# A mask's table moved ahead of a LayerNorm's power on GpSimd, and a PSUM copy moved ahead of exponentials on ScalarE

## The chip, the cores and the metric

One core of one Trainium2 chip. The metric is the device time of one launch in microseconds (us), median of several runs. Where a kernel is compared with another by a ratio, both ran on the same chip in the same rounds. A ratio is the mean time of one kernel's runs over that of the other's of the same rounds, so it is not quite the ratio of the medians quoted beside it.

## The reference, cut to what matters

128 graphs with 128 nodes and 512 features go through two layers, each with a residual and a LayerNorm: a graph attention with 8 heads and a mask from the adjacency, then two hypergraph convolutions with a LayerNorm between them.

```python
# layer 0: attention
dense = leaky_relu(e_self[..., :, None] + e_neigh[..., None, :], 0.2)
dense = dense + NEG_BIG * (1.0 - A[:, None, :, :])       # the mask: 0 or -1e10
att = softmax(dense, axis=-1)
x = layernorm(x + relu(att @ feats + b))                  # "first LayerNorm"
# layer 1: hypergraph convolutions
h = layer_norm(relu(hypergraph_conv(x, adj, W1, b1)))     # "first convolution"
x = layernorm(x + hypergraph_conv(h, adj, W2, b2) + x)
```

## The kernel before

The kernel takes graphs in 64 pairs. Each step of a pair has a lag (in turns of the loop) and a time within the turn; all steps of all pairs are sorted by `(pair + lag) * 38.6 + time`, and every engine gets its instructions in that order. So a turn mixes work of five pairs (lags 0 to 4). What the change and the argument touch:

```python
    @step(0, 38.4)                                   # GpSimd: the mask's table, once per pair
    def mask(p, s):
        s["neg"] = work.tile([P, 2, N], F32, tag="neg", name=f"neg_{p}", bufs=2)
        nc.gpsimd.tensor_scalar(s["neg"], s["a"], -1.0, BIG, op0=ALU.add, op1=ALU.mult)
    ...
    for (g, q), tm, (lag, tl), (lagx, tx), te, tt in (
        ((0, 0), 31.0, (1, 33.2), (1, 36.1), 2.7, 18.1), ((0, 1), 32.2, ..., 4.6, 18.15),
        ((1, 0), 34.2, ..., 7.8, 21.5), ((1, 1), 35.4, ..., 7.9, 21.55),
    ):
        at(1, tm, masked, g, q)                      # GpSimd: scores += neg   ("nb", L576)
        at(2, te, exponential, g, q)                 # ScalarE: 4 exponentials ("nb", L606)
    ...
    # GpSimd: h_means 30.62 ("m"), rstds "a" 30.8 (first LayerNorm's power, "rsa"),
    #         h_rstd 36.0 (second power, "rsh"), z_sums 2.7, 3.4, 4.1, 4.8 ("zS", L780)
    # VectorE: y_scale 0.6 and 1.3 (two SBUF inputs, "y<-y,rsh,bw_bc", L909)
    ...
    # TensorE, first convolution as seven products; X, Y, W are PSUM banks:
    # product 1 -> X (2.0), 2 -> Y (3.8), 6 adds into X (5.6), 5 -> W (7.35), 7 adds into X ...
    # product 6 reads zS[1]; copy 0 empties X (ScalarE, 4.0, L329) before product 6 adds into it
    chain("ph", 3, (2.0, 3.8, 5.6, 7.35, 9.1, 12.65, 14.4, 4.0, 7.5, 11.0), hidden, HALF)
```

## Time and profile before

| | before |
|---|---|
| time, median of 3 runs | 2561.94 us (2559.85 to 2563.33) |
| span of the profiled run, clock granted to TensorE (1 is full speed) | 2559.9 us, 0.997 |
| TensorE matmul / weight loads busy | 98% / 89% |
| one turn of the loop | 39.21 us |
| stall of TensorE in a turn, by starts of weight loads | 0.56 us |

Read it as a kernel whose TensorE is almost full, with one short wait that returns in 61 of the 64 turns. That the wait matters shows in part 4 of the page, the chain that ended last (the work followed back from the last instruction, at each step to what released it): TensorE is only two thirds of it, and GpSimd has a quarter.

```profile
PE 66%; POOL 23%; issue 8%; DVE 2%; DMA 1%; ACT 0%; SPq 0%; POOLq 0%; DVEq 0%; ACTq 0%
```

### The profile page before, as it was taken

What the parts mean: (1) busy time and instruction counts of PE and PEld (TensorE: products, weight loads), DVE (VectorE), ACT (ScalarE), POOL (GpSimd) and SP (SyncE); (2) the same over time, 40 slices, a digit from 0 to 9 for tenths busy, and PEclk for the clock granted to TensorE, in tenths of its full rate; (3) what the DMA queues carried; (4) which work ended last, traced back from release to release, by engine and by line L of the source; (5) the groups of instructions that cost most, each with busy time, mean ns of one, the idle gap of its engine ahead of it and who ended that gap; (6) DMA issues with size and microseconds to landing.
All of it is one profiled execution on the core that took longest, in us unless ns stands there. A gap on an engine that the chain in (4) does not pass through costs nothing.

```text
span 2559.9 us, 48549 instructions
## 1 busy us (share of the span) xinstructions
PE 2516.7 (98%) x16349; PEld 2275.8 (89%) x16349; DVE 1914.3 (75%) x4332; ACT 1539.8 (60%) x4481; POOL 1832.7 (72%) x2058
## 2 busy tenths in 40 slices
PE   7999999999999999999999999999999999999998
PEld 5899889998998998989989988999899999898997
DVE  7877777777777777777777777777777777777765
ACT  4565665655756656657556566565575665665753
POOL 5777777776777677767777777777677767776774
PEclk9999999999999999999999999999999999999999
DMA  6544444444444444454454444444444444444431
GB/s 184 134 137 134 135 139 141 134 125 145 129 133 141 133 141 135 127 150 130 126 147 133 134 136 138 141 134 124 147 128 133 141 133 141 136 130 148 130 108 54
DMA packets 420840, 343.76 MB, mean 134 GB/s; under 512 B 141272, under 2 KB 370160, under 8 KB 420592
## 3 DMA queue, kind: packets, MB, share of 16 engines
q1 hardware_dynamic: 417120, 336.19, 44.4%
q10 hardware_dynamic: 3472, 4.47, 0.5%
q8 instruction: 131, 2.15, 0.3%
q14 instruction: 117, 0.96, 0.1%
HBM read 238.83 MB, written 101.71 MB: 133 GB/s over the span
## 4 chain that ended last, share of the span: by engine, by line
PE 66%; POOL 23%; issue 8%; DVE 2%; DMA 1%; ACT 0%; SPq 0%; POOLq 0%; DVEq 0%; ACTq 0%
PE phX L792 14%; POOL nb L576 11%; PE pyX L473 9%; PE phW L792 9%; PE pfX L473 9%; PE pav L662 8%; POOL zS L780 4%; PE pq L919 4%; PE pyY L473 4%; PE pfW L473 4%; POOL neg L363 2%; PE pfY L473 2%; POOL rsh L905 2%; POOL rsa L709 2%; DVE y L876 1%
## 5 line engine op out<-in xcount | busy, mean ns | idle before, releaser
L792 PEld LDWEIGHTS phX<-zS,w_sb 128*128 128x128 f32 x3072 | 362.8, 192 | 61.5 <-issue 31.1
L792 PE MATMUL phX<-zS,w_sb 128*128 128x128 f32 x3072 | 380.7, 277 | 19.0 <-POOL zS L780 17.2
L329 ACT COPY py<-pyX 128x257 f32<-128x257 f32 x189 | 70.8, 375 | 539.2 <-PE pyX L473 526.4
L845 POOL TENSOR_TENSOR sq<-sq 128x512 f32<-128x512 f32 (+2 forms) x384 | 343.9, 896 | 23.7 <-ACT sq L833 0.5
L576 POOL TENSOR_TENSOR nb<-nb,neg 128x512 f32<-128x512 f32 x256 | 318.2, 1275 | 13.5 <-DMA nb<-rd 13.5
L592 ACT ACTIVATE nb<-nb,ft 128x128 f32<-128x128 f32 x1020 | 317.7, 391 | 6.8 <-POOL nb L576 6.8
L606 ACT ACTIVATE nb<-nb,nm 128x128 f32<-128x128 f32 x1024 | 319.9, 393 | 0.4 <-DVE nm L598 0.4
L598 DVE TENSOR_REDUCE nm<-nb 128x4 f32<-128x512 f32 x256 | 174.6, 683 | 179.5 <-ACT nb L592 117.4
L709 POOL TENSOR_TENSOR rso<-veo,mhalf 128x2 f32<-128x2 f32 x63 | 44.1, 700 | 332.9 <-DVE veo L707 332.9
L662 PEld LDWEIGHTS pav<-ft,eT 128*128 128x128 f32 x2048 | 248.3, 192 | 8.4 <-DVE eT L639 0.8
L662 PE MATMUL pav<-ft,eT 128*128 128x65 f32 x2048 | 242.5, 272 | 0.0
L473 PE MATMUL pyX<-w_sb,hS 128*128 128x257 f32 x1008 | 242.5, 382 | 0.0
L473 PE MATMUL pyX<-w_sb,h 128*128 128x257 f32 x1008 | 239.5, 379 | 0.5 <-ACT py L329 0.5
L822 ACT ACTIVATE h<-h,vecs 128x128 f32<-128x128 f32 x768 | 238.4, 392 | 2.2 <-DVE h L807 2.2
L473 PE MATMUL pyW<-w_sb,hS 128*128 128x256 f32 x1008 | 238.6, 378 | 0.3 <-DVE y L876 0.3
L473 PEld LDWEIGHTS pyW<-w_sb,hS 128*128 128x128 f32 x1008 | 190.7, 189 | 27.9 <-DVE y L876 0.7
L686 POOL TENSOR_TENSOR y<-y,b_bc 128x512 f32<-128x512 f32 x128 | 162.5, 1270 | 67.6 <-DVE y L677 67.6
L473 PEld LDWEIGHTS pyX<-w_sb,h 128*128 128x128 f32 x1008 | 186.4, 190 | 25.5 <-ACT py L329 0.9
L473 PEld LDWEIGHTS pyX<-w_sb,hS 128*128 128x128 f32 x1008 | 186.1, 190 | 24.3
L627 DVE STREAM_TRANSPOSE eT<-eb 128x512 f32<-128x512 f32 x252 | 163.1, 684 | 0.8 <-DMA eb<-ed 0.7
L833 ACT ACTIVATE sq<-h 128x512 f32<-128x512 f32 x256 | 160.7, 629 | 2.1
L455 POOL TENSOR_TENSOR hS<-h 128x512 f32<-128x512 f32 x126 | 158.6, 1277 | 2.3 <-ACT h L822 2.3
(167 smaller groups left out, 5669.2 us busy)
## 6 DMA issues: line engine op xcount, KB each, us to landing
nb<-rd SPq DMA_DIRECT2D x127, 512.0 KB, 6.6
ed<-nb SPq DMA_DIRECT2D x126, 512.0 KB, 2.6
eb<-ed SPq DMA_DIRECT2D x504, 128.0 KB, 2.9
x<-in_x_dram SPq DMA_DIRECT2D x64, 512.0 KB, 9.4
out_dram<-o SPq DMA_DIRECT2D x63, 512.0 KB, 2.8
xb<-in_x_dram SPq DMA_DIRECT2D x248, 128.0 KB, 3.0
a<-in_adj_dram SPq DMA_DIRECT2D x64, 128.0 KB, 8.1
w<-in_adj_dram SPq DMA_DIRECT2D x128, 64.0 KB, 7.4
```

What stands on the lines that cost most here:

```text
L473: nc.tensor.matmul(to[:, :n], lhs[:, k, :], rhs[:, k, :n], start=bool(start) and k == 0, stop=(k == nk - 1), skip_group_check=True,)
L576: nc.gpsimd.tensor_tensor(t, t, neg[:, :, None, :].to_broadcast([P, NB, HH, B]), op=ALU.add)
L592: nc.scalar.activation(t, t, AF.Prelu, bias=s["ft"][:, g, h, 0:1], alpha=SLOPE)
L598: nc.vector.tensor_reduce(s["nm"][:, g, hs], scores(p, s, g, hs).rearrange("p b h j -> p h b j"), AX.XY, ALU.max, negate=True,)
L606: nc.scalar.activation(t, t, AF.Exp, bias=s["nm"][:, g, h:h + 1])
L627: nc.vector.transpose(s["eT"][:, g, hs, :].rearrange("p h (b i) -> p h b i", b=NB), s["eb", g][:, :, hs, :].rearrange("p b h j -> p h b j"),)
L662: nc.tensor.matmul(t[:, h * (U + 1):(h + 1) * (U + 1)], s["eT"][:, g, q * HH + h, :], s["ft"][:, g, q * HH + h, 2:], start=True, stop=True,)
L686: nc.gpsimd.tensor_tensor(s["y"][:, g, :], s["y"][:, g, :], b0_bc, op=ALU.add)
L792: nc.tensor.matmul(to[:, m * N:(m + 1) * N], w[:, k, m * P:(m + 1) * P], rhs[:, k, :], start=bool(start) and m == 0 and k == 0, stop=(k == ...
L822: nc.scalar.activation(dst[:, k, :], src[:, k, :], AF.Relu, bias=b1_sb[:, c:c + 1])
L833: nc.scalar.activation(s["sq"][:, g, q * KH // 2:(q + 1) * KH // 2, :], hid(s, g, q), AF.Square, scale=DH ** -0.5,)
L845: nc.gpsimd.tensor_tensor(t[:, :n, :], t[:, :n, :], t[:, n:2 * n, :], op=ALU.add)
```

## The change

The intent: the mask's table is not urgent, yet it stood between the second power and the differences zS for which TensorE waits. It goes into a gap in which GpSimd waits anyway. And the copy that the same TensorE product needs no longer stands behind four exponentials.

```diff
-    @step(0, 38.4)
+    @step(0, 30.63)
     def mask(p, s):
...
-        ((0, 0), 31.0, (1, 33.2), (1, 36.1), 2.7, 18.1), ...
+        ((0, 0), 31.0, (1, 33.2), (1, 36.1), 4.05, 18.1), ...
```

More of the change, by code (lines that the diff above doesn't have):

```diff
@@ L643 @@
     for (g, q), tm, (lag, tl), (lagx, tx), te, tt in (
-        ((0, 0), 31.0, (1, 33.2), (1, 36.1), 2.7, 18.1), ((0, 1), 32.2, (1, 35.0), (1, 36.7), 4.6, 18.15),
+        ((0, 0), 31.0, (1, 33.2), (1, 36.1), 4.05, 18.1), ((0, 1), 32.2, (1, 35.0), (1, 36.7), 4.6, 18.15),
         ((1, 0), 34.2, (2, 2.05), (2, 2.1), 7.8, 21.5), ((1, 1), 35.4, (2, 6.0), (2, 7.3), 7.9, 21.55),
```

## The prediction

> **What bounds the kernel now.** I read the page first, then the table of waits, then the chain that ended last, then the timeline of one steady turn of the loop (64 pairs of graphs; one turn is 39.21 us, from the chain's step to GpSimd's mask at 1314.26 us to the same step at 1353.47). Part 1 of the page:
>
> ```profile
> PE 2516.7 (98%) x16349; PEld 2275.8 (89%) x16349; DVE 1914.3 (75%) x4332; ACT 1539.8 (60%) x4481; POOL 1832.7 (72%) x2058
> ```
>
> TensorE (PE, with its weight loads PEld) is the bound; the question is only where it still stands. The table of waits (total us, times, longest) names one wait that returns every turn, and beside it an engine that has time to spare:
>
> ```profile
> PEld phX L792 <- POOL zS L780: 28.8, 61, 0.5
> POOL rsa L709 <- DVE vea L707: 151.1, 64, 3.3
> ```
>
> The first: in 61 turns TensorE waits for the difference that GpSimd (POOL) makes (zS). The second: GpSimd itself sat idle 2.36 us in the mean (151.1 / 64) before the first LayerNorm's power. The chain that ended last (start us, length us, what) joins the two:
>
> ```profile
> 1304.54 0.34 POOL m L894 x2
> 1304.88 2.37 issue
> ...
> 1307.28 0.70 POOL rsa L709
> 1307.98 2.17 POOL nb L576 x2
> ...
> 1314.26 0.96 POOL neg L363
> 1315.22 1.14 POOL zS L780
> ...
> 1316.43 0.74 POOL zS L780
> ...
> 1317.21 2.05 PE phX L792 x16
> ```
>
> So GpSimd idles 2.37 us, makes the power, adds the mask four times, makes the second power, then the next pair's mask table (neg, 0.96 us), and only then the two differences for which TensorE stands. The loads of weights in the timeline show how long it stands (start us, length, then the group):
>
> ```profile
> 1313.09 1.86 PEld L792 LDWEIGHTS phX<-zT,w_sb 128*128 128x128 f32 x16
> 1314.87 1.87 PEld L792 LDWEIGHTS phY<-zT,w_sb 128*128 128x128 f32 x16
> 1317.21 1.86 PEld L792 LDWEIGHTS phX<-zS,w_sb 128*128 128x128 f32 x16 [0.48 <-POOL zS L780]
> 1318.99 1.87 PEld L792 LDWEIGHTS phW<-zS,w_sb 128*128 128x128 f32 x16
> ```
>
> Like groups start 1.78 us apart (1314.87 - 1313.09, 1318.99 - 1317.21), these two 2.34. **The stall is 0.56 us a turn**; the 0.48 in brackets is less, since ends are modelled. Over 61 turns it is 34 us, 1.3% of the time, and no other wait of TensorE in the table returns each turn. This is the most that the change can win in the loop.
>
> **What the Trainium skill says.** "Perfetto Trace Analysis", section "Identifying the Most-Contended Engine", says that matmul busy time says little of the distance to the roofline and that weight-load time is to be used; here both are high (98% and 89%), and I measure the stall on the loads for that reason. "SBUF — State Buffer", section "SBUF: two separate sides", says that VectorE with two SBUF inputs, or in a two-port mode, and GpSimd take a shared pair of ports as a lock for a whole instruction, and the other is blocked. The trace agrees:
>
> ```profile
> 1319.73 0.84 DVE L745 SCALAR_TENSOR_TENSOR o<-y,b_bc 128x512 f32<-128x512 f32 x1
> 1319.98 1.18 POOL L455 TENSOR_TENSOR xS<-xT 128x256 f32<-128x256 f32 x1
> 1320.50 1.21 DVE L745 SCALAR_TENSOR_TENSOR o<-y,b_bc 128x512 f32<-128x512 f32 x1
> 1321.12 1.18 POOL L455 TENSOR_TENSOR xS<-xT,xS 128x256 f32<-128x256 f32 x1
> ```
>
> Here the two engines take turns: a GpSimd difference that takes 0.73 us elsewhere takes 1.18, and a VectorE step that takes 0.66 alone takes 1.21. "ScalarE: Activation LUTs", section "Table sets: the hidden batching unit", says that cheap functions, copy among them, are in every table set; the trace has a single table load (1.28 us, at the start), so a copy between two other functions should cost no reload.
>
> **Part 1, the mask's table.** It removes the 0.96 us between the second power (rsh) and the first difference (zS), and puts it between the means (m, end 1304.88) and the first power (start 1307.28). It adds no instruction. Alone it takes 0.42 us, as one early instance shows, against 0.96 beside VectorE's two-input step L909:
>
> ```profile
> 33.16 0.42 POOL L363 TENSOR_SCALAR neg<-a 128x256 f32<-128x256 f32 x1
> 1305.39 0.66 DVE L693 SCALAR_TENSOR_TENSOR y<-y,x 128x512 f32<-128x512 f32 x1
> 1314.21 1.55 DVE L909 SCALAR_TENSOR_TENSOR y<-y,rsh,bw_bc 128x512 f32<-128x512 f32 x2 [0.85 <-POOL rsh L905]
> ```
>
> In its new place it runs from about 1304.95 beside VectorE's transpose (L370, 1.10 us whether GpSimd works or not) and should end at 1305.38, just as the residual L693 starts. At worst it waits for L693 and ends at 1306.5, still before the power. Its data are there: the adjacency was loaded some 30 us earlier, and the buffer it writes was last read a turn before. So the power and all behind it keep their time.
>
> But the first difference does not win the full 0.96. It now meets L909, whose two steps start at 1314.21, where the mask met it before. I replay the turns of the lock with the durations of the L745 pair. First step of L909 to about 1314.9; first zS issued 1314.26, held up, 1.18 long, ends 1315.44; second step of L909 waits for it and ends about 1316.09 (1314.88 + 1.21); second zS issued 1315.50 behind its predecessor, held up again, ends at 1316.68. Before it ended at 1317.17. So of the 0.96 only **0.49 arrives**. TensorE's load may start at 1316.73 (0.05 later, as before) and would like to at 1314.87 + 1.78 = 1316.65. Stall 0.08 in place of 0.56: **0.48 us a turn**, times 61 = 29 us.
>
> **Part 2, the copy.** ScalarE's order and TensorE's matching limit:
>
> ```profile
> 1313.82 1.28 ACT L592 ACTIVATE nb<-nb,ft 128x128 f32<-128x128 f32 x4
> 1315.01 1.27 ACT L606 ACTIVATE nb<-nb,nm 128x128 f32<-128x128 f32 x4
> 1316.17 0.57 ACT L329 COPY ph<-phX 128x512 f32<-128x512 f32 x1
> ```
>
> The same stalled group adds into the bank that this copy empties, so it must wait for the copy's end, 1316.74. Today that is hidden behind zS (1317.17). With part 1 alone both arrive at about the same time, 1316.7, so the copy would hold TensorE some 0.1 us. With part 2 the copy starts when the first product ends (its matmuls run 1313.14 to 1315.14), ends at about 1315.76, and has 0.9 us to spare. ScalarE pays a wait of some 0.17 us (from 1315.01 to 1315.18) and its next copy moves to 1319.4, still 0.9 us ahead of the group at about 1320.3 that needs it. On its own part 2 wins nothing; with part 1 it protects some 0.1 us a turn, already in the 0.48.
>
> **The sum.** 61 x 0.48 = 29 us; the start and the tail (last 60 us) have their own waits, and I count nothing there. 2562 - 29 = **2533 us**, 1.1% less; a turn of 38.73 us.
>
> **The rivals.**
> 1. The stall goes wholly: second zS before 1316.65, for instance if GpSimd gets the lock first (0.73 + 0.08, then 1.18: end 1316.25). Against: L909 starts 0.05 us before GpSimd's step now. It would give 61 x 0.56 = 34 us: 2528.
> 2. VectorE becomes the limit a little later. L909's second step ends 0.33 us later, and L745 starts about 0.17 later, behind ScalarE; by the same replay L745 ends at 1322.05 in place of 1321.71, while TensorE comes 0.48 us sooner. For: 0.8 us of VectorE's margin go there. Against: the next reader in a hurry (the second use of bank W, 1325.6 after the change) finds its sum ready at about 1324.75, and the transposes for the attention (end of the first about 1331.3) have 0.9 us before TensorE's group at 1332.20. If part of it were to bite, a new wait of 0.1 to 0.3 us would leave 11 to 23 us: 2539 to 2551.
> 3. The mask collides with L693 and delays the power by up to 0.4 us, which delays the four masked adds and also the first output that ScalarE makes for TensorE. Against: the 0.42 us alone ends before L693 starts. It would leave about 0.1 us a turn: some 2556.
> 4. The first turns: for the fourth pair the adjacency load is issued at 85.16 and the mask would run at about 90.5, before its old place at 98.65. A late landing costs at most some 2 us once.
>
> **Range and chances.** The middle is the replay, 2533. The low end is rival 1 with 2 us for the start and scatter between runs: 2526. The high end gives rival 2 or 3 a partial bite, a stall of about 0.27 left: 61 x 0.29 = 18, so 2544. Faster by over 2% needs 51 us, more than the stall holds: 0.01. Slower by over 2% needs a new stall of 0.8 us in each turn: 0.01. Within 2%: 0.98.
>
> **What would show it.** Right: GpSimd's wait before rsa falls from 2.40 to about 1.9 us with neg in it at about 0.42; the first and second zS take about 1.18 each, and the second step of L909 about 1.2; the wait of phX for zS shrinks to under 0.1 us or goes; the copy stands before the exponentials; turns of 38.65 to 38.8 us; neg leaves the chain. Wrong: turns still over 39, a wait of phX for ScalarE's copy, a wait of pav or phW for VectorE, neg at 0.9 us or more and rsa later against the end of pyY, or a lower granted clock.

## The result, and the profile after

| | before | after |
|---|---|---|
| time, median | 2560.89 us (4 runs) | 2526.86 us (4 runs, 2526.64 to 2528.03) |
| ratio | | 0.9867, 95% interval 0.985 to 0.9884 |
| one turn | 39.21 us | 38.67 us |
| stall in a turn | 0.56 us | 0 |

The time fell by 34.0 us, 1.3%: within 2%, inside the predicted range of 2526 to 2544 us but close to its low end, 6 us below the predicted middle. Parts 1 and 4 of the page after:

```profile
PE 2498.3 (99%) x16349; PEld 2270.5 (90%) x16349; DVE 1920.5 (76%) x4332; ACT 1539.4 (61%) x4481; POOL 1789.9 (71%) x2058
PE 97%; DVE 1%; DMA 1%; POOL 0%; issue 0%; ACT 0%; SPq 0%; POOLq 0%; DVEq 0%; ACTq 0%
```

The chain that ended last is now TensorE almost alone, where GpSimd had 23%; GpSimd is also 43 us less busy (1832.7 to 1789.9), though it does the same work. One turn of the timeline after, GpSimd and VectorE first, then ScalarE, then the weight loads (start us, length us, engine, group; in brackets the idle time before it):

```profile
1286.80 0.40 POOL L363 TENSOR_SCALAR neg<-a 128x256 f32<-128x256 f32 x1
1289.12 0.70 POOL L709 TENSOR_TENSOR rsa<-vea,mhalf 128x2 f32<-128x2 f32 x1 [1.92 <-DVE vea L707]
1295.99 0.73 POOL L780 TENSOR_TENSOR zS<-zT 128x256 f32<-128x256 f32 x1
1296.05 2.34 DVE L909 SCALAR_TENSOR_TENSOR y<-y,rsh,bw_bc 128x512 f32<-128x512 f32 x2 [0.85 <-POOL rsh L905]
1296.79 1.06 POOL L780 TENSOR_TENSOR zS<-zT,zS 128x256 f32<-128x256 f32 x1
1297.01 0.58 ACT L329 COPY ph<-phX 128x512 f32<-128x512 f32 x1
1297.49 2.45 ACT L606 ACTIVATE nb<-nb,nm 128x128 f32<-128x128 f32 x8
1296.70 1.87 PEld L792 LDWEIGHTS phY<-zT,w_sb 128*128 128x128 f32 x16
1298.48 1.87 PEld L792 LDWEIGHTS phX<-zS,w_sb 128*128 128x128 f32 x16
```

The mask takes 0.40 us in the gap, and the power still waits 1.92 us behind it. The weight loads start 1298.48 - 1296.70 = 1.78 us apart: no stall. The second zS ends at 1297.85, 0.63 before TensorE asks; the copy ends at 1297.59, 0.89 before. Note the two starts in the middle: zS at 1295.99, VectorE's L909 at 1296.05. GpSimd goes first now. The prediction had VectorE first. (The profile's own legend calls GpSimd's spans rough, so the main reading of them, in e7, is also made from starts alone.)

### The profile page after: what moved, and what is told of

Read it like the earlier page. It is cut to its first block, busy times and chain, and to the rows that moved or that the text cites. A ratio compares the mean times of both kernels' runs of the same rounds, so it can differ in the third digit from the quotient of the medians.

```text
span 2525.1 us, 48492 instructions
## 1 busy us (share of the span) xinstructions
PE 2498.3 (99%) x16349; PEld 2270.5 (90%) x16349; DVE 1920.5 (76%) x4332; ACT 1539.4 (61%) x4481; POOL 1789.9 (71%) x2058
## 4 chain that ended last, share of the span: by engine, by line
PE 97%; DVE 1%; DMA 1%; POOL 0%; issue 0%; ACT 0%; SPq 0%; POOLq 0%; DVEq 0%; ACTq 0%
PE phX L792 18%; PE pyX L473 17%; PE phW L792 9%; PE pfX L473 9%; PE pav L662 9%; PE pyW L473 8%; PE phY L792 4%; PE pz L757 4%; PE pq L919 4%; PE pfW L473 4%; PE pyY L473 4%; PE pfY L473 2%; PE pd L429 1%; PE pf L510 1%; PE pm L887 1%; PE py L962 0%
## 5 line engine op out<-in xcount | busy, mean ns | idle before, releaser
L792 PEld LDWEIGHTS phX<-zS,w_sb 128*128 128x128 f32 x3072 | 363.1, 192 | 33.0 <-issue 31.6
L792 PE MATMUL phX<-zS,w_sb 128*128 128x128 f32 x3072 | 374.4, 275 | 2.4 <-POOL xS L455 1.2
L606 ACT ACTIVATE nb<-nb,nm 128x128 f32<-128x128 f32 x1024 | 313.4, 392 | 0.4 <-DVE nm L598 0.4
L909 DVE SCALAR_TENSOR_TENSOR y<-y,rsh,bw_bc 128x512 f32<-128x512 f32 x126 | 148.5, 1217 | 52.9 <-POOL rsh L905 52.9
```

The source lines that it names most:

```text
L606: nc.scalar.activation(t, t, AF.Exp, bias=s["nm"][:, g, h:h + 1])
L792: nc.tensor.matmul(to[:, m * N:(m + 1) * N], w[:, k, m * P:(m + 1) * P], rhs[:, k, :], start=bool(start) and m == 0 and k == 0, stop=(k == ...
```

## The experiments

The theory to be tested has three statements. (a) What counts is the end of the second zS against the moment at which TensorE asks for it, and what stands on GpSimd between the second power and zS; the place to which the mask goes is free. (b) The copy is a second limit close behind; each part alone gets only as far as the other limit. (c) VectorE's L909 and GpSimd take turns on a shared pair of ports, instruction by instruction, so the order in which they start decides how long zS takes. The rivals: the filled gap itself is the gain; the copy did nothing; durations only add up, with no part played by VectorE.

The stall of each run is read from its weight loads in one steady turn: start of the phX load on zS, minus start of the phY load before it, minus 1.78. The last column checks it: 2527 + 61 x stall.

| run | difference from before | phY, phX loads start (us) | stall (us) | median (us) | ratio to before | 2527 + 61 x stall |
|---|---|---|---|---|---|---|
| before | | 1314.87, 1317.21 | 0.56 | 2560.89 | | 2561 |
| e1_after_again | the change | 1296.70, 1298.48 (first trace of the change) | 0 | 2527.12 | 0.9872 | 2527 |
| e2_part1_only | mask moved only | 1303.30, 1305.29 | 0.21 | 2539.89 | 0.992 | 2540 |
| e3_part2_only | copy moved only | 1312.61, 1314.94 | 0.55 | 2559.2 | 1.0001 | 2561 |
| e4_mask_after_zS | copy; mask behind zS | 1336.52, 1338.31 | 0.01 | 2527.67 | 0.9873 | 2528 |
| e5_small_op_1 | change + 1 tiny step | 1301.70, 1303.61 | 0.13 | 2533.87 | 0.9897 | 2535 |
| e6_small_op_2 | change + 2 tiny steps | 1311.25, 1313.46 | 0.43 | 2553.68 | 0.9973 | 2553 |
| e7_scale_later | copy; L909 later; mask in old place | 1336.50, 1338.29 | 0.01 | 2527.2 | 0.9871 | 2528 |
| e8_mask_twice_old | mask twice in old place | 1325.35, 1328.05 | 0.92 | 2583.65 | 1.0092 | 2583 |
| e9_adj_seen_early | load waited for earlier | 1314.62, 1316.98 | 0.58 | 2561.73 | 1.0001 | 2562 |
| e10_neg_three_buffers | third buffer for neg | 1314.73, 1317.07 | 0.56 | 2561.71 | 1.0001 | 2561 |

One wait, read from one turn, accounts for all eleven times within 2 us. All runs were correct.

### e1_after_again: the change again

No edit. 

> The changed kernel once more, as the yardstick for the other three runs of this call. Both theories: about 2527 us, ratio to the kernel before 0.987, turns of 38.66 us and no wait of TensorE for zS.

As expected: 2527.12 us (interval of the ratio 0.9858 to 0.9885).

### e2_part1_only: the mask alone

```diff
 # against the changed kernel
-        ((0, 0), 31.0, (1, 33.2), (1, 36.1), 4.05, 18.1), ...
+        ((0, 0), 31.0, (1, 33.2), (1, 36.1), 2.7, 18.1), ...
```

> Mask moved, copy left behind the exponentials. My theory (two limits stood close behind one another): the stalled TensorE group now waits for ScalarE's copy, which ends at 1316.74 in the frame of the turn before, 0.05 later the load starts at 1316.79 in place of 1316.65: a stall of 0.14 us a turn, 61 turns, 8 us: 2533 to 2538 us, and the waits name ScalarE's copy. Rival (the copy had enough time anyway, part 2 does nothing): 2527 us, as the full change.

Measured 2539.89 us: the rival (2527) falls, and the cost is half as large again as I expected (just above my 2533 to 2538), 12.8 us over e1, 0.21 us a turn. One turn of its timeline:

```profile
1303.39 1.06 POOL L780 TENSOR_TENSOR zS<-zT,zS 128x256 f32<-128x256 f32 x1
1304.61 0.57 ACT L329 COPY ph<-phX 128x512 f32<-128x512 f32 x1
1303.30 1.87 PEld L792 LDWEIGHTS phY<-zT,w_sb 128*128 128x128 f32 x16
1305.29 1.86 PEld L792 LDWEIGHTS phX<-zS,w_sb 128*128 128x128 f32 x16
```

zS is ready at 1304.45; the copy ends at 1305.18, and the load starts 0.11 later. I had allowed 0.05 from the copy's end, the distance that I saw between zS and the load; ScalarE's release took twice that. The table of waits doesn't name this wait: it has phX waiting for the copy only twice in all, so that without the starts of the loads one would look for it in vain.

### e3_part2_only: the copy alone

```diff
 # against the changed kernel
-    @step(0, 30.63)
+    @step(0, 38.4)
     def mask(p, s):
```

> Mask left in its old place, copy ahead of the exponentials. My theory: zS still comes last, the wait stays at 0.56 us a turn: 2557 to 2563 us, same as before. Rival (the copy was part of the stall or ScalarE's new order frees something): at least 5 us faster than before.

2559.2 us, ratio 1.0001 (0.9988 to 1.0015): nothing. Mask and zS run as in the kernel before, and the stall is 0.55. Together with e2: part 1 alone wins 20 us, part 2 alone none, both 33. The parts are not a sum; each lifts one of two limits.

### e4_mask_after_zS: another place for the mask

```diff
 # against the changed kernel
-    @step(0, 30.63)
+    @step(1, 5.5)
     def mask(p, s):
```

> Mask behind the four differences zS, still ahead of the next turn's use, copy first. Not in GpSimd's idle gap at all, only off the stretch between the second power and zS. Theory that only the stretch before zS counts: 2526 to 2530 us, like the full change, though GpSimd's idle gap before the first power stays 2.4 us. Rival (the filled gap is what gains): 2545 us or more.

2527.67 us, the same as the full change, with the gap left empty. Its mask, and its power with the idle time that the change fills:

```profile
1328.94 0.70 POOL L709 TENSOR_TENSOR rsa<-vea,mhalf 128x2 f32<-128x2 f32 x1 [2.40 <-DVE vea L707]
1339.58 0.40 POOL L363 TENSOR_SCALAR neg<-a 128x256 f32<-128x256 f32 x1
```

So filling the gap is a safe place, not the source of the gain.

### e5_small_op_1 and e6_small_op_2: the order at the ports

```diff
 # against the changed kernel, at the end of h_rstd (GpSimd)
         nc.gpsimd.tensor_tensor(s["rs", "h"], ve, mhalf, op=ALU.pow)
+        junk = small.tile([P, 2], F32, tag="junk", name=f"junk_{p}")
+        nc.gpsimd.tensor_scalar(junk, ve, 0.0, EPS, op0=ALU.max, op1=ALU.add)
+        nc.gpsimd.tensor_scalar(junk, junk, 0.0, EPS, op0=ALU.max, op1=ALU.add)   # e6 only
```

> The changed kernel with one more tiny GpSimd step (128x2, 0.22 us elsewhere) between the second power and the first zS, so that VectorE's L909 has its ports first. Theory of the lock's order: VectorE now goes first, zS is held up behind both steps of L909, the second zS ends 0.7 to 0.9 us later than in the changed kernel, over the 0.6 us to spare: a stall of 0.1 to 0.3 us a turn, 2533 to 2546 us. Rival (times only add up: 0.22 and a gap of 0.09 on top): the second zS ends 0.3 us later, within the 0.6 us to spare, no stall: 2526 to 2528 us.

> Two such tiny steps in a row. Theory of the lock's order: stall of 0.1 to 0.45 us a turn, 2533 to 2555 us; it need not grow by the second step's own 0.3 us, as a held-up zS absorbs it. Rival (times add up): the second zS 0.6 us later, on the edge of what is to spare: 2526 to 2531 us.

2533.87 and 2553.68 us: both inside what the order at the ports gives, both outside what adding up gives. They were run on another chip. First e5, then e6 (the added lines shift L909 to L911 in e5 and to L912 in e6):

```profile
1301.02 0.22 POOL L907 TENSOR_SCALAR junk<-veh 128x2 f32<-128x2 f32 x1
1301.08 1.89 DVE L911 SCALAR_TENSOR_TENSOR y<-y,rsh,bw_bc 128x512 f32<-128x512 f32 x2 [0.86 <-POOL rsh L905]
1301.19 1.22 POOL L780 TENSOR_TENSOR zS<-zT 128x256 f32<-128x256 f32 x1
1302.49 1.06 POOL L780 TENSOR_TENSOR zS<-zT,zS 128x256 f32<-128x256 f32 x1
```

```profile
1310.55 0.22 POOL L907 TENSOR_SCALAR junk<-veh 128x2 f32<-128x2 f32 x1
1310.60 1.41 DVE L912 SCALAR_TENSOR_TENSOR y<-y,rsh,bw_bc 128x512 f32<-128x512 f32 x2 [0.86 <-POOL rsh L905]
1310.85 0.58 POOL L908 TENSOR_SCALAR junk<-junk 128x2 f32<-128x2 f32 x1
1311.39 1.21 POOL L780 TENSOR_TENSOR zS<-zT 128x256 f32<-128x256 f32 x1
1312.68 0.72 POOL L780 TENSOR_TENSOR zS<-zT,zS 128x256 f32<-128x256 f32 x1
```

In e5 the tiny step starts ahead of VectorE and takes its 0.22 us; then VectorE's first step is at the ports, and zS takes 1.22 instead of 0.73. In e6 the second tiny step, 0.22 us of work at most, meets that first step and takes 0.58; the first zS then meets VectorE's second step and takes 1.21; the second zS meets nobody and takes 0.72. A step on two numbers a partition cannot need 0.58 us for its data: it was held. (My expectation that the second step might cost less than its own time was wrong: e6 lost 20 us more than e5, as it, too, was held.)

### e7_scale_later: VectorE out of the way

```diff
 # against the changed kernel (mask back in its old place)
-    @step(0, 30.63)
+    @step(0, 38.4)
     def mask(p, s):
...
-    at(4, 0.6, y_scale, 1, until=LAST)
-    at(4, 1.3, y_scale, 0, until=LAST)
+    at(4, 5.95, y_scale, 1, until=LAST)
+    at(4, 5.96, y_scale, 0, until=LAST)     # likewise for the last pair but one
```

> Mask in its OLD place, copy first, and VectorE's L909 (two-input) moved behind the sum of the first hidden block, so that nothing of VectorE with two SBUF inputs runs beside mask and zS. Theory (the ports' lock made up half of the old stall): mask 0.42 in place of 0.96, first zS 0.73 in place of 1.16, the second zS ends about 1 us sooner, before TensorE asks for it: 2526 to 2534 us without moving the mask. Rival (the serial length of GpSimd's work is what counts, not the meeting with VectorE): about 2561 us as before, or at most 5 us faster.

It was run on another chip. 2527.2 us, with the mask exactly where it was before:

```profile
1335.90 0.40 POOL L363 TENSOR_SCALAR neg<-a 128x256 f32<-128x256 f32 x1
1336.27 0.73 POOL L780 TENSOR_TENSOR zS<-zT 128x256 f32<-128x256 f32 x1
1337.07 0.73 POOL L780 TENSOR_TENSOR zS<-zT,zS 128x256 f32<-128x256 f32 x1
```

Mask and first zS take 0.40 and 0.73 us where they took 0.96 and 1.16: 0.99 us less, and none of it is less work. The starts say the same without any end: from the mask to the second zS it is 1.17 us (1335.90 to 1337.07) in place of 2.17 (1314.26 to 1316.43). This is the strongest result. More than half of the mask's apparent cost, and over a third of the first zS's, was VectorE's; moving either side of the meeting removes the stall. L909 starts at 1339.27 there and pays in its new place (2.28 us for two), where it has time.

### e8_mask_twice_old: the old place, doubled

```diff
 # against the kernel before
         nc.gpsimd.tensor_scalar(s["neg"], s["a"], -1.0, BIG, op0=ALU.add, op1=ALU.mult)
+        nc.gpsimd.tensor_scalar(s["neg"], s["a"], -1.0, BIG, op0=ALU.add, op1=ALU.mult)
```

> The kernel before, with the mask's table made twice in its old place. If the old place is on the path that sets the turn: each turn longer by 0.4 to 0.9 us, 61 turns: 2585 to 2616 us. If the old place had slack: about 2561 us.

2583.65 us, just under the range. It was run on another chip. The second mask and the first zS (L364 and L781 here):

```profile
1325.78 0.72 POOL L364 TENSOR_SCALAR neg<-a 128x256 f32<-128x256 f32 x1
1326.46 0.72 POOL L781 TENSOR_TENSOR zS<-zT 128x256 f32<-128x256 f32 x1
```

The old place is on the path, but a second mask of 0.72 us (plus a gap of 0.09) adds only 0.36 us of stall. With it ahead, the first zS no longer meets L909 and takes 0.72 instead of 1.16, which gives 0.44 back: 0.72 + 0.09 - 0.44 = 0.37.

### e9_adj_seen_early and e10_neg_three_buffers: why the mask starts late

In the kernel before, the mask starts at 1314.26, 0.09 us behind the end of the second power (1313.46 + 0.71), and VectorE's L909 at 1314.21 is ahead of it; in the changed kernel zS starts 0.03 before that end, ahead of L909. Two guesses at the cause:

```diff
 # e9, against the kernel before: a tiny GpSimd read of the adjacency ahead of the first power
+    @step(0, 30.63)
+    def seen(p, s):
+        t = small.tile([P, 2], F32, tag="seen", name=f"seen_{p}")
+        nc.gpsimd.tensor_scalar(t, s["a"][:, 0, :2], 0.0, EPS, op0=ALU.max, op1=ALU.add)
 # e10, against the kernel before: tag "neg" with
-        bufs=2
+        bufs=3
```

> The kernel before, with one tiny GpSimd step (128x2) in the idle gap ahead of the first power that reads the adjacency, so that the mask itself, still in its old place, no longer has to wait for that load. Theory: the mask starts 0.09 us behind the end of the second power, where zS starts 0.03 ahead of it, because it carries a wait for its load; with the wait met earlier it starts 0.1 us sooner, ahead of L909, takes the ports first (0.42 long), and the stall falls from 0.56 to 0.2 to 0.45 us a turn: 2540 to 2555 us. Rival (the 0.09 belongs to the mask's step or its buffer, not to the load): no change, 2558 to 2562 us, the mask still 0.09 behind and 0.96 long.

> The kernel before with three buffers for the mask's table in place of two, the mask in its old place. Theory that the reuse of its buffer delays the mask's start: mask 0.1 us sooner, ahead of L909, 2540 to 2555 us. Rival (the load or the step itself): no change, 2558 to 2562 us, the mask still starts 0.09 behind the power and takes 0.96 us.

Both 2561.7 us, ratio 1.0001: no change. In the trace of e9 the mask starts at 1314.02, still 0.05 behind VectorE's L909 at 1313.97, and takes 0.97 us; in e10 1314.11 against 1314.06, and 0.97. Neither an earlier wait for its load nor a third buffer moves its start. In every trace where I looked (before, after, e4, e7, e8, e9, e10) it starts about 0.09 us behind the end of its predecessor, whatever that is; why stays open (a zS that depends on its predecessor starts about as far behind it, 0.07 to 0.08 us). It isn't the operation as such: the tiny step of e5, also a TENSOR_SCALAR, starts 0.02 before its predecessor's end.

## Why the prediction was right, point by point

- **The bound and the size of the stall: right.** 61 x 0.56 = 34 us was named as the most that the loop could give; 34.0 us came. No other wait of TensorE for an engine returned; the idle time of its weight loads that the table puts down to "issue" (31.1 and 29.9 us before) stayed as it was (31.6 and 30.1).
- **Part 1, the new place: right.** The mask was to take 0.42 us there and leave some 1.9 us of idle time; it takes 0.40 and leaves 1.92. Rival 3, a later power, did not occur.
- **Part 1, the old place: the step that failed is "First step of L909 to about 1314.9; first zS issued 1314.26, held up".** I took the mask's start, 0.09 behind the power, for the start that zS would have in its place. zS starts 0.12 sooner, ahead of L909. So the first zS runs free (0.73), only the second is held (1.06), and it ends 0.63 us before it is needed, where I had it 0.03 too late (1316.68 against 1316.65) and, with the 0.05 to the load, left 0.08 us of stall. That is rival 1, for which I had named 2528 and the same order (0.73, then 1.18). So the range held because rival 1 set its low end, not because the replay was right: of its signs, the first zS of about 1.18 us did not come. e5 shows that the taking of turns was sound and the order wrong: give VectorE the first turn, and a stall of 0.13 comes back.
- **Part 2: right in kind, too small in size.** Nothing on its own (e3: 0), a protection beside part 1. I put it at some 0.1 us a turn; e2 against e1 gives 0.21 (12.8 us / 61), for the release after the copy took 0.11 us and not 0.05.
- **Rival 2, VectorE as the next limit: did not bite.** L909 became slower than foreseen, 2.34 us for two in place of 1.55, where the replay gave 1.88 (1314.21 to 1316.09): with GpSimd first, both its steps are held (1.21 and 1.22). But the differences xS, made sooner, meet L745 and L420 less: the two steps of L745 take 1.82 us in place of 1.98, the two scalings of L420 0.47 in place of 0.94. TensorE has no wait for VectorE in the loop.
- **The kind: right.** The stall holds 1.3%, so "within 2%" was all but certain.

No version beat the change: e4 and e7 reach the same 2527 us, since TensorE is 96 to 97% of the chain in all of them, and what it still waits for lies in the first turns and at the end (in the changed kernel before 100 us and after 2480).

## What to carry to other kernels

Where a nearly full engine stalls a little in every turn, measure the stall by the starts of equal instructions; the table of waits undersized it here (28.8 us in 61 turns, 0.47 of 0.56) and in e2 did not name it at all. Then ask which instructions on the late engine, between the last moment it truly waited and the result, are not for that result: they can go off that stretch. Here two such places, a wait ahead of it and one behind it, did equally well; others were not tried. Look also at who runs beside the stretch: over half of a GpSimd step's length (here 0.56 of 0.96 us) was VectorE's turn at the ports, and the cure can lie on either engine.

## What the Trainium skill lacked or had wrong

- "SBUF — State Buffer", section "Who interferes with whom": its whole-instruction lock, and that the order of issue decides who blocks, agree with the traces of the change, e5, e6 and e7 (a 128x2 step of GpSimd 0.22 us free and 0.58 held; zS 0.73 free, up to 1.22 held). It lacks how little decides: with both engines released by the same power, VectorE starts 0.06 us behind zS after the change and 0.11 ahead of it in e5, and TensorE's stall is 0 or 0.13 us a turn (e5 has the tiny step's own 0.2 us in it too).
- The same section goes through copy, cast, tensor_scalar, tensor_tensor and tensor_reduce to say which can grab the shared pair, but not through block transposes, nor does it say whether one has a two-port mode. Here a GpSimd mask of 0.40 us ran wholly beside VectorE's 1.10 us transpose L370, neither longer than without the other (mask 0.40 in e7, L370 1.10 in e4).
- "GPSIMD Engine Reference", section "2.1 Instruction dispatch", says that the completion of one GpSimd instruction holds back only what waits for it. The trace agrees (zS starts 0.03 us before the power's end, a dependent zS 0.07 to 0.08 behind its source's end), but no page that I read gives these figures, nor what makes the mask start 0.09 behind a predecessor that it doesn't read; e9 and e10 didn't find it.
- No page that I read gives the time from a result to TensorE's next load: 0.05 us from GpSimd's zS, 0.11 us from ScalarE's PSUM copy (e2).
- "ScalarE: Activation LUTs", section "Table sets: the hidden batching unit": nothing wrong was seen. With the copy between two other functions the trace still has a single table load of 1.28 us; what a switch of sets costs in all no run here shows.
